# A wide state-space layer: its first norm on one copy of each token, the residual sum moved one stage on

## The chip, the cores and the metric

The kernel runs on one core of a Trainium2 chip. The metric is the device time of one execution in microseconds (us), from start to end, on that core; lower is better. The engines are named as in the profile: PE (matrix multiplication; PEld are its weight loads), DVE (vector), ACT (activation functions and copies out of PSUM), POOL (general elementwise work, which reads and writes SBUF), and SP, which here only issues DMAs. Each engine runs its own instructions in order; semaphores order the engines among each other.

## The reference

The input is `x` of 4 images x 64 channels x 128 x 128 pixels, in float32. Four layers follow one another. Only the last one is touched; in it each image is a sequence of 16,384 tokens with 64 features:

```python
y = relu(conv2d(x, conv1_w, conv1_b)); y = conv2d(y, conv2_w, conv2_b)
t = y.reshape(Bn, C, Hh * Ww).transpose(0, 2, 1)
t = t + mamba(layernorm(t, ln1_w, ln1_b), ...)
t = t + pvt2ffn(layernorm(t, ln2_w, ln2_b), Hh, Ww, ...)
y = t.transpose(0, 2, 1).reshape(Bn, C, Hh, Ww)
return x + y          # x: the layer's own input
```

`mamba` projects the normalised tokens to 128 inner channels and 128 gates, runs a causal depthwise convolution of 4 taps and silu over the sequence, derives a step size delta (softplus) and, for each token, 64 numbers B and 64 numbers C, and then for each of the 128 x 64 (channel, state) pairs runs the recurrence

```python
h = h * exp(delta * A) + (delta * u) * B
y = sum over states of h * C
```

before it multiplies by silu(gate) and projects back to 64 features. `pvt2ffn` is a feed-forward block: 64 to 256 features, a 3 x 3 depthwise convolution, gelu, back to 64.

## The kernel before

Five functions run one after the other: `layer0` (a small state-space layer with 16 states), `layer1`, `layer2_convs3` (which ends with the two convolutions of the last layer; it writes the layer's input to the DRAM tensor x3 and the tokens to t3), `layer3_mamba` (t3 to s3 and n3) and `layer3_ffn` (n3 and s3 to the output).

**`layer3_mamba`** cuts the tokens into 64 chunks of TC = 1024. Channels lie on the partitions. A chunk is 16 groups of 4 states, each group 4 iterations, so 64 iterations per chunk and 4096 in all. In each iteration (`_Mamba.run`) DVE runs one scan (L626) over a 128 x 1024 tile: the decay `da` comes from ACT (L582), the input `bx` from PE in PSUM, the result goes into one of 8 ring slots. POOL multiplies the ring slot by C (L632, tile `cb`, loaded by DMA, L421). PE adds the products of a group up into `y` (L457) some 3 iterations after the group's last scan; only then is the ring slot free for the scan 8 iterations later. There are two kinds of group. For kind A (10 of 16) ACT (L431) and POOL (L435) prepare scaled copies which PE transposes into `bx` (L514). For kind D (6 of 16) PE spreads B over the partitions (L520) and DVE multiplies `bx` by `du` (L526). PSUM holds three `bx` tiles and one `y` tile; the helper steps below `take` one of the three and `give` it back, which leaves the scans two.

**The order** is fixed by the program: each engine's instructions stay in the order in which they are written (`_Pin`). The helper steps for the next chunk (`ahead`) and for the last one (`behind`) are generators. `yield m.slot(c, name)` continues at the end of a given iteration; `yield "next", 0` continues in the next iteration. Counted within a chunk of 64, the steps stand at: project 9, centre2 11, norm2 13 (of the chunk just ended), centre 21, norm 23, conv 32, z 34, v 36, duT 43, C 53, B 55 (of the next chunk).

**`ahead`** is the first norm. The convolution on PE treats two taps at once: rows 0 to 63 of its input S hold the tokens shifted by one column against rows 64 to 127, which hold them as they are. The kernel before loads t3 twice into X, shifted and unshifted (L1353 or L1356, and L1357), and norms both copies: centring matmul (L300 with K.cent), copy with scale and square on ACT (L1375, L1376), mean matmul, logarithm and exponential (L140, L141), and a product on POOL into S (L1385), all of them on 128 x 1024 elements. Two columns are carried from chunk to chunk in `tail` (L1365, L1388). `front` then runs convolution (L300 with cw), gate and step size.

**`behind`** loads the tokens t3 and the layer's input x3 of the finished chunk, projects y and adds the tokens in PSUM (L672), copies the sum (L1402), adds x3 on POOL (L1404), norms again on 128 x 512 elements (two halves of the 1024 tokens on the two halves of the partitions; L1411, L1412, L140, L141, L1421), and stores tokens plus x3 in s3 (L1423) and the normed tokens in n3 (L1424).

**`layer3_ffn`** works in 32 strips of 16 image rows. Per strip it loads n3 (with `first`) and s3 (`res`), runs the depthwise convolution partly on PE (L1584) and partly on DVE (L1530), and adds `res` at the end (L1551). POOL sets border columns there and nothing else. Its tiles have two buffers.

All DMAs concerned are issued by SP, in program order; a DMA that has to wait stops those behind it.

Of the kernel before, what the change touches and what calls it, by code (L numbers as in the profile page):

```python
# [10 lines left out]
F32 = mybir.dt.float32  # L11
# [6 lines left out]
P = 128  # L18
B, C, HH, WW = 4, 64, 128, 128
HW = HH * WW  # L20
TC = 1024
NH = TC // 512
# [89 lines left out]
def _halves(ap, t0):  # L112

    return [ap[:, t0 + 512 * h : t0 + 512 * (h + 1)] for h in range(NH)]
# [660 lines left out]
def _gradients(ctx, tc, K, x1, out):  # L775
# [9 lines left out]
    with tc.tile_pool(name="sob", bufs=2) as sp, tc.tile_pool(name="sobc", bufs=1) as sc, tc.tile_pool(  # L785
# [5 lines left out]
        for b in range(B):  # L791
            img = x1[b].rearrange("c (h r w) -> (c h) r w", h=2, w=C)
            for r0 in range(0, HH, R):
                X = sp.tile([P, R + 2, C], F32, name="X", tag="X")
                h = sp.tile([P, R + 2, C + 1], F32, name="h", tag="h")
# [8 lines left out]
                for i, e in ((at, mid), (mid, to)):  # L804
                    nc.sync.dma_start(X[:, i:e, :], img[:, lo + i - at : lo + e - at, :])
                    nc.scalar.copy(h[:, i:e, 0:1], X[:, i:e, 0:1])
                    nc.scalar.copy(h[:, i:e, C : C + 1], X[:, i:e, C - 1 : C])
# [519 lines left out]


@with_exitstack
def layer3_mamba(ctx, tc, K, w, t3, x3, s3, n3):  # L1330

    nc = tc.nc
    slots = {"centre": -43, "norm": -41, "conv": -32, "z": -30, "v": -28, "B": -9, "duT": -21, "C": -11}
    slots |= {"project": 73, "centre2": 75, "norm2": 77}
    m = _Mamba(ctx, tc, K, 64, w, "DADAADAADADAADAA", {"xc": 1, "sz": 2, "tmp": 4, "bc": 1, "soon": (8, 20, 52), "da": 7, "made": 7}, slots)
    cp = m.cp
    eps = cp.tile([P, 1], F32, name="eps3")
    nc.vector.memset(eps, 1e-5)
    woT = cp.tile([P, 64], F32, name="woT")
    nc.sync.dma_start(woT, w["out_wT"])  # L1340

    g1, b1 = (_dup(nc, cp, w[k], f"{k}_") for k in ("ln1_w", "ln1_b"))
    m.shift(b1)
    pad = cp.tile([P, 1], F32, name="pad")
    nc.vector.tensor_scalar_mul(pad, b1, -1.0)

    tail = cp.tile([P, 2], F32, name="tail")

    def load(c):
        b, t0 = c["at"]  # L1350
        X = c["X"] = m.t("X", 1)
        if t0:
            nc.sync.dma_start(X[:64], t3[b, :, t0 - 1 : t0 - 1 + TC])  # L1353
        else:
            nc.gpsimd.memset(X[:64, 0:1], 0.0)  # L1355
            nc.sync.dma_start(X[:64, 1:], t3[b, :, : TC - 1])  # L1356
        nc.sync.dma_start(X[64:], t3[b, :, t0 : t0 + TC])  # L1357

    def ahead(c):
        if c is chunks[0]:  # L1360
            load(c)
        t0 = c["at"][1]
        S = m.t("S", 1, TC + 2)
        if t0:
            nc.gpsimd.tensor_copy(S[:, :2], tail)  # L1365
        else:
            nc.gpsimd.tensor_copy(S[:, :2], pad.to_broadcast([P, 2]))
        xs, sq = m.tmp("nxc"), m.tmp("nsq")
        yield m.slot(c, "centre")
        pm = m.take()  # L1370
        m.mm(pm, (K.cent, c["X"]))
        if c is not chunks[-1]:
            load(chunks[c["no"] + 1])
        yield "next", 0
        nc.scalar.activation(xs, pm, AF.Copy, scale=g1)  # L1375
        nc.scalar.activation(sq, pm, AF.Square)  # L1376
        m.give(pm)
        yield m.slot(c, "norm")
        pm = m.take()
        m.mm(pm, (K.j2, sq))  # L1380
        yield "next", 0
        _rstd(nc, sq, pm, eps)
        m.give(pm)
        yield "next", 0
        nc.gpsimd.tensor_mul(S[:, 2:], xs, sq)  # L1385
        if not t0:
            nc.gpsimd.tensor_copy(S[:64, 2:3], pad[:64])
        nc.gpsimd.tensor_copy(tail, S[:, TC:])  # L1388
        yield from m.front(c, S, lambda: None)

    def behind(c, yg):
        b, t0 = c["at"]
        tx = m.tmp("tx")
        tr, xr = tx[:, :512], tx[:, 512:]
        for h in range(NH):
            nc.sync.dma_start(tr[64 * h : 64 * (h + 1)], _halves(t3[b], t0)[h])
            nc.sync.dma_start(xr[64 * h : 64 * (h + 1)], _halves(x3[b], t0)[h])
        yield m.slot(c, "project")
        pm = m.take(1)
        m.project(pm, woT, yg, tr)  # L1400
        yield "next", 0
        nc.scalar.copy(tr, pm)  # L1402
        m.give(pm)
        nc.gpsimd.tensor_add(xr, xr, tr)  # L1404
        yield m.slot(c, "centre2")
        pm = m.take(1)
        m.mm(pm, (K.cent, tr))
        yield "next", 0
        no = m.tmp("no")
        xs, o = no[:, :512], no[:, 512:]  # L1410
        nc.scalar.copy(xs, pm)  # L1411
        nc.scalar.activation(o, pm, AF.Square)  # L1412
        m.give(pm)
        yield m.slot(c, "norm2")
        pm = m.take(1)
        m.mm(pm, (K.j2, o))
        yield "next", 0
        _rstd(nc, o, pm, eps)
        m.give(pm)
        yield "next", 0  # L1420
        nc.gpsimd.tensor_mul(o, xs, o)  # L1421
        for h in range(NH):
            nc.sync.dma_start(_halves(s3[b], t0)[h], xr[64 * h : 64 * (h + 1)])  # L1423
            nc.sync.dma_start(_halves(n3[b], t0)[h], o[64 * h : 64 * (h + 1)])  # L1424

    chunks = [{"at": (b, t0), "reset": t0 == 0} for b in range(B) for t0 in range(0, HW, TC)]
    m.run(chunks, ahead, behind, 48)


@with_exitstack  # L1430
def layer3_ffn(ctx, tc, K, w, n3, s3, out):

# [1 line left out]
    nc = tc.nc  # L1436
    R = 16
    HR = (R + 2) // 2
    NK = R // 8
    half = [slice(64 * h, 64 * (h + 1)) for h in range(2)]  # L1440
    cp = ctx.enter_context(tc.tile_pool(name="ffc", bufs=1))
    wp = ctx.enter_context(tc.tile_pool(name="ffw", bufs=2))
# [121 lines left out]
    for n, (b, r0) in enumerate(strips):  # L1564
        simg = s3[b].rearrange("c (r w) -> c r w", w=WW)
        h0 = H[0]
        H = {}
        ahead = first(*strips[n + 1], H) if n + 1 < len(strips) else iter(())
        next(ahead, None)

        res = wp.tile([P, NK, 4, WW], F32, name="res3", tag="res3")
        for q in range(R // 4):
            nc.sync.dma_start(res[half[q % 2], q // 2], simg[:, r0 + 4 * q : r0 + 4 * q + 4, :])

        g0 = [wp.tile([P, NK, 4, WW], F32, name=f"g0{i}", tag=f"g0{i}") for i in range(2)]
        o = wp.tile([P, NK, 4, WW], F32, name="o3", tag="o3")
        for kk in range(NK):
            pd = [dp.tile([P, 4, WW], F32, name=f"pd{i}", tag=f"pd{i}") for i in range(2)]
            for k in range(9):
                dy, dx = divmod(k, 3)  # L1580
                for h in range(2):
                    r = 8 * kk + 4 * h + dy
                    for i in range(2):
                        nc.tensor.matmul(  # L1584
                            pd[i][half[h]],
                            diag[half[i], k, :],
                            h0[half[i], r : r + 4, dx : dx + WW],
                            start=k == 0,
                            stop=k == 8,
                        )  # L1590
                if k % 3 == 2:
                    next(ahead, None)
                if (kk, k) == (0, 3) and owed:
                    second(*owed)
                    more(rest, 1)
                if (kk, k) == (1, 3):
                    second(n, g0, g1, res, o, 0)
                    more(rest, 4)
                pin()
            for i in range(2):  # L1600
                nc.scalar.activation(g0[i][:, kk], pd[i], AF.Gelu, bias=dwb[:, i : i + 1])
            if not kk:
                nc.scalar.activation(g1, g1, AF.Gelu, bias=dwb1)
                rest = taps(H[1]) if 1 in H else iter(())
                g2 = more(rest, 4)
            pin()
        owed, g1 = (n, g0, g1, res, o, 1), g2
# [59 lines left out]
@with_exitstack  # L1667
def kernel(ctx, tc, w, cst, x, out):
    nc = tc.nc
    dp = ctx.enter_context(tc.tile_pool(name="dram", bufs=1, space=DRAM))  # L1670
    x1, x2, x3, t3, s3, n3 = (
        dp.tile([B, C, HW], F32, name=f"d_{n}") for n in ("x1", "x2", "x3", "t3", "s3", "n3")
    )
    for upto, layer, *of in (
        ("sel", layer0, w["l0"], x, x1),
        (None, layer1, w["l1"], x1, x2),
        (None, layer2_convs3, w["l2"], w["l3"], x2, x3, t3),
        ("sel", layer3_mamba, w["l3"], t3, x3, s3, n3),
        ("eye", layer3_ffn, w["l3"], n3, s3, out),
    ):  # L1680
        with tc.tile_pool(name="const", bufs=1) as kp:
            layer(tc, _Consts(nc, kp, cst, upto), *of)
# [26 lines left out]
```

## Time and profile before

| what | us |
|---|---|
| median of 3 runs | 17,647.88 (17,646.33 to 17,652.58) |
| profiled execution, its own time | 17,656.56 |
| its span, first to last instruction | 17,654.7 |
| first to last scan of `layer3_mamba` | 5,501.8 to 16,689.3 |
| from one chunk to the next, mean (median) | 174.9 (174.5) |

| per chunk of `layer3_mamba` | rows of the profile |
|---|---|
| scan L626, DVE, 64 times | 2327 ns each, one every 2.25 us |
| multiplication L526, DVE, 24 times | 1209 ns each, one every 1.12 us |
| ring product L632, POOL, 64 times | 2382 ns each, one every 2.3 us |
| first norm, ACT: L1375, L1376, L140, L141 | 1115, 1016, 1101, 1058 ns |
| first norm, POOL: L1385, L1388, L1365 | 2419, 185, 190 ns |
| residual sum, POOL: L1404 | 1290 ns |

The span is that of the profiled execution; its own time is 1.9 us longer, and the median of the other runs 8.7 us shorter. An instruction's duration overlaps the next one's start a little, so that on a full engine the distance of two starts is the better price.

### The profile page before, as it was taken

The page shows a single profiled execution, that of the slowest core. Times are in us where ns is not written, and L with a number is a line of the kernel's source. Part 1 is how long each engine was busy: PE and PEld are TensorE (multiplying, and loading weights), DVE is VectorE, ACT ScalarE, POOL GpSimd, SP SyncE. Part 2 cuts the span into 40 slices and gives each one's busy share as a digit, 9 for nine tenths or more (in the row PEclk, how much of TensorE's full clock was granted, in tenths as well). Part 3 has the DMA queues.
Part 4 walks back from the last instruction along what each step waited for, and adds up shares of the span by engine and source line. Part 5 has one row for each costly group of instructions (what it writes and reads, how often), then busy time and mean ns, then how long its engine had stood idle before and what let it go on. Part 6 is the DMA issues. An engine that isn't in the chain of part 4 may idle for free. (4 is left out here: it accounts for less than half of the span.)

```text
span 17654.7 us, 242673 instructions
## 1 busy us (share of the span) xinstructions
PE 14230.1 (81%) x82490; PEld 6984.1 (40%) x82490; DVE 15333.9 (87%) x8623; ACT 14311.2 (81%) x29985; POOL 13820.2 (78%) x7966
## 2 busy tenths in 40 slices
PE   7888888798997777777777777777777777777799
PEld 3333333387334333333333333333333333333333
DVE  8999999522216999999999999999999999999977
ACT  8999999112335999999999999999999999999733
POOL 7999999200005999999999999999999999999700
PEclk8888888799998999999999999999999999999899
DMA  6766666111212333333333333333333333333222
GB/s 160 179 179 178 175 179 177 51 61 45 72 41 79 89 90 91 88 93 85 93 85 94 83 95 84 94 86 91 87 91 86 93 87 91 89 90 91 69 59 55
DMA packets 669699, 1723.23 MB, mean 98 GB/s; under 512 B 196816, under 2 KB 232096, under 8 KB 661024
## 3 DMA queue, kind: packets, MB, share of 16 engines
q1 hardware_dynamic: 668448, 1707.69, 36.0%
q8 instruction: 646, 10.58, 0.3%
q14 instruction: 605, 4.96, 0.1%
HBM read 1434.33 MB, written 272.63 MB: 97 GB/s over the span
## 5 line engine op out<-in xcount | busy, mean ns | idle before, releaser
L632 POOL TENSOR_TENSOR ring<-ring,cb 128x1024 f32<-128x1024 f32 x5120 | 12038.9, 2381 | 335.4 <-DVE ring L626 186.1
L626 DVE TENSOR_TENSOR_SCAN ring<-da,state,bx 128x1024 f32<-128x1024 f32 x4848 | 11053.0, 2327 | 70.8 <-PE y L457 38.1
L431 ACT ACTIVATE bxT<-duT,BT 128x128 f32<-128x128 f32 x21504 | 6706.0, 389 | 29.9 <-PE bx L514 28.1
L582 ACT ACTIVATE da<-dl,A 128x1024 f32<-128x1024 f32 x5120 | 5751.0, 1139 | 168.1 <-DVE ring L626 115.2
L514 PE MATMUL bx<-cst,bxT 128*128 128x128 f32 x24576 | 3693.7, 300 | 945.1 <-DVE ring L626 641.6
L514 PEld LDWEIGHTS bx<-cst,bxT 128*128 128x128 f32 x24576 | 3248.7, 209 | 2341.9 <-DVE ring L626 1523.1
L520 PE MATMUL bx<-bc,spread 64*128 64x512 f32 (+1 forms) x8192 | 2401.2, 684 | 1439.2 <-DVE ring L626 1427.9
L457 PE MATMUL y<-ring,cst 128*32 128x512 f32 x20480 | 3030.3, 675 | 120.8 <-POOL ring L632 120.1
L526 DVE TENSOR_TENSOR bx<-du,bx 128x1024 f32<-128x1024 f32 x2048 | 2463.1, 1211 | 301.3 <-PE bx L520 183.8
L520 PEld LDWEIGHTS bx<-bc,spread 64*128 64x128 f32 (+1 forms) x8192 | 690.2, 195 | 2819.0 <-DVE ring L626 2305.6
L457 PEld LDWEIGHTS y<-ring,cst 128*32 128x32 f32 x20480 | 633.3, 119 | 2040.0 <-issue 1433.7
L1197 PE MATMUL cv<-img,cw 64*64 64x512 f32 x9216 | 1009.3, 595 | 73.2 <-DMA img<-d_x 45.5
L300 PE MATMUL bx<-S,cw 128*128 128x512 f32 x1024 | 663.2, 806 | 367.9 <-DVE ring L626 354.5
L1355 POOL MEMSET X<- 64x1 f32 x4 | 0.4, 97 | 1122.2 <-DMA cw<-in_l_conv_wT 1122.2
L435 POOL TENSOR_TENSOR bxT<-duT,BT 128x512 f32<-128x512 f32 x768 | 808.3, 1053 | 10.1 <-ACT BT L381 10.1
L1122 POOL TENSOR_TENSOR xs<-xs,cl 128x1024 f32<-128x1024 f32 x32 | 76.0, 2374 | 860.8 <-DVE cl L1121 860.8
L1496 POOL MEMSET h<- 128x18 f32 x64 | 8.3, 132 | 875.2 <-PE pd L1584 443.5
L1197 PEld LDWEIGHTS cv<-img,cw 64*64 64x64 f32 x9216 | 435.1, 134 | 645.5 <-issue 537.8
L1510 ACT ACTIVATE h<-ph,ff_fc_b 128x384 f32<-128x384 f32 (+1 forms) x384 | 201.1, 578 | 593.2 <-PE ph L1505 593.2
L1584 PE MATMUL pd<-h,diag 64*64 64x512 f32 x4608 | 632.0, 603 | 0.7 <-issue 0.7
L626 DVE TENSOR_TENSOR_SCAN ring<-da,bx 128x1024 f32<-128x1024 f32 x272 | 604.8, 2268 | 9.4 <-PE y L457 5.8
L1530 DVE SCALAR_TENSOR_TENSOR g<-h,dww,g 128x2048 f32<-128x2048 f32 x256 | 601.9, 2351 | 11.0
(314 smaller groups left out, 9963.3 us busy)
## 6 DMA issues: line engine op xcount, KB each, us to landing
cb<-c SPq DMA_DIRECT2D x5120, 128.0 KB, 2.8
dl<-d SPq DMA_DIRECT2D x2048, 128.0 KB, 3.3
du<-d SPq DMA_DIRECT2D x2048, 128.0 KB, 3.7
d<-pos SPq DMA_DIRECT2D x128, 512.0 KB, 3.7
d<-u SPq DMA_DIRECT2D x128, 512.0 KB, 3.9
X<-d_t SPq DMA_DIRECT2D x124, 256.0 KB, 4.1
S<-in_x SPq DMA_DIRECT2D x120, 256.5 KB, 4.5
res<-in_x SPq DMA_DIRECT2D x128, 128.0 KB, 3.0
```

The costliest lines, as they stand in the source:

```text
L300: self.nc.tensor.matmul(out[: l.shape[1], k : k + 512], l, r[:, k : k + 512], start=i == 0, stop=i == len(pairs) - 1)
L431: nc.scalar.activation(t[:, k, q].rearrange("p e j -> p (e j)"), c["duT"][:, k, :], AF.Copy, scale=c["BT"][:, k, n : n + 1])
L435: nc.gpsimd.tensor_mul(t[:, k].rearrange("p q e j -> p q (e j)"), c["duT"][:, k].unsqueeze(1).to_broadcast(shape), c["BT"][:, k, NQ * g : ...
L457: nc.tensor.matmul(c["y"][DD * j : DD * (j + 1), _COLS[h]], K.sel, hc[:, _COLS[h]], start=False, stop=u["g"] == self.ng - 1,)
L514: nc.tensor.transpose(bx[:, P * m : P * (m + 1)], v["bxT"][:, m, :, :, j].rearrange("p q e -> p (q e)"), self.K.eye)
L520: nc.tensor.matmul(bx[:, _COLS[h]], self.spread[v["g"]][r], self.rows(v["c"]["B"], h, 0), start=True, stop=True)
L526: nc.vector.tensor_mul(tiles[k], v["c"]["du"][j], tiles[k])
L582: nc.scalar.activation(das[nexp], v["c"]["dl"][k], AF.Exp, scale=self.A[:, k, v["g"] : v["g"] + 1])
L626: nc.vector.tensor_tensor_scan(hs, das.pop(i), tiles[i], 0.0 if u["c"].get("reset") else st, ALU.mult, ALU.add)
L632: nc.gpsimd.tensor_mul(hc, hs, u["cb"])
L1197: nc.tensor.matmul(p[i][half[h]], W[half[i], k, :], src[half[i], at : at + 4, dx : dx + WW], start=k == 0, stop=k == 8,)
L1584: nc.tensor.matmul(pd[i][half[h]], diag[half[i], k, :], h0[half[i], r : r + 4, dx : dx + WW], start=k == 0, stop=k == 8,)
```

## The change

**First norm (`ahead`).** Each token is loaded and normed once. X becomes 128 x 512: the first 512 tokens on partitions 0 to 63, the next 512 on partitions 64 to 127. Centring, scaling, squaring, mean, logarithm, exponential and the product run on 512 columns and end in the tile `nx` (one buffer of the shared kind `tmp` where there were two). The norm takes a half of a PSUM tile. S then gets 3 leading columns from `tail` and is filled by four DMAs from SBUF to SBUF, each of 64 partitions x 512 columns: both halves, once for each of the two shifts. `tail` is taken from the last columns of `nx` by two small copies. The DMAs are issued two iterations after POOL's product.

**Residual sum.** `layer3_mamba` no longer reads x3; s3 holds the tokens without it. `layer3_ffn` loads x3 beside s3 (four DMAs a strip, tile `xin`) and POOL adds the two, 128 x 1024 elements a strip.

```diff
-    tail = cp.tile([P, 2], F32, name="tail")
+    tail = cp.tile([P, 3], F32, name="tail")
+    nc.vector.memset(tail, 0.0)
...
-        X = c["X"] = m.t("X", 1)
-        if t0:
-            nc.sync.dma_start(X[:64], t3[b, :, t0 - 1 : t0 - 1 + TC])
-        else:
-            nc.gpsimd.memset(X[:64, 0:1], 0.0)
-            nc.sync.dma_start(X[:64, 1:], t3[b, :, : TC - 1])
-        nc.sync.dma_start(X[64:], t3[b, :, t0 : t0 + TC])
+        X = c["X"] = m.t("X", 1, 512)
+        for h, src in enumerate(_halves(t3[b], t0)):
+            nc.sync.dma_start(X[64 * h : 64 * (h + 1)], src)
...
-        S = m.t("S", 1, TC + 2)
-        if t0:
-            nc.gpsimd.tensor_copy(S[:, :2], tail)
-        else:
-            nc.gpsimd.tensor_copy(S[:, :2], pad.to_broadcast([P, 2]))
-        xs, sq = m.tmp("nxc"), m.tmp("nsq")
+        S = m.t("S", 1, TC + 3)
+        no = m.tmp("nx")
+        xs, sq = no[:, :512], no[:, 512:]
         yield m.slot(c, "centre")
-        pm = m.take()
+        pm = m.take(0)
...
         yield m.slot(c, "norm")
-        pm = m.take()
+        pm = m.take(0)
         m.mm(pm, (K.j2, sq))
...
-        nc.gpsimd.tensor_mul(S[:, 2:], xs, sq)
-        if not t0:
-            nc.gpsimd.tensor_copy(S[:64, 2:3], pad[:64])
-        nc.gpsimd.tensor_copy(tail, S[:, TC:])
+        nc.gpsimd.tensor_mul(xs, xs, sq)
+        nc.gpsimd.tensor_copy(S[:, :3], tail if t0 else pad.to_broadcast([P, 3]))
+        for h in range(2):
+            nc.gpsimd.tensor_copy(tail[64 * h : 64 * (h + 1), : 3 - h], xs[64:, 509 + h :])
+        yield "next", 0
+        yield "next", 0
+        for k in range(2):
+            for h in range(NH):
+                at = 3 - k + 512 * h
+                nc.sync.dma_start(S[64 * k : 64 * (k + 1), at : at + 512], xs[64 * h : 64 * (h + 1)])
         yield from m.front(c, S, lambda: None)
...
-        tx = m.tmp("tx")
-        tr, xr = tx[:, :512], tx[:, 512:]
+        tr = m.tmp("tx")[:, :512]
         for h in range(NH):
             nc.sync.dma_start(tr[64 * h : 64 * (h + 1)], _halves(t3[b], t0)[h])
-            nc.sync.dma_start(xr[64 * h : 64 * (h + 1)], _halves(x3[b], t0)[h])
...
-        nc.gpsimd.tensor_add(xr, xr, tr)
...
-            nc.sync.dma_start(_halves(s3[b], t0)[h], xr[64 * h : 64 * (h + 1)])
+            nc.sync.dma_start(_halves(s3[b], t0)[h], tr[64 * h : 64 * (h + 1)])
...
+        ximg = x3[b].rearrange("c (r w) -> c r w", w=WW)
+        xin = wp.tile([P, NK, 4, WW], F32, name="xin", tag="xin")
         for q in range(R // 4):
             nc.sync.dma_start(res[half[q % 2], q // 2], simg[:, r0 + 4 * q : r0 + 4 * q + 4, :])
+            nc.sync.dma_start(xin[half[q % 2], q // 2], ximg[:, r0 + 4 * q : r0 + 4 * q + 4, :])
+        nc.gpsimd.tensor_add(res, res, xin)
```

More of the change, by code (lines that the diff above doesn't have):

```diff
@@ L1329, in layer3_mamba @@
 @with_exitstack
-def layer3_mamba(ctx, tc, K, w, t3, x3, s3, n3):
+def layer3_mamba(ctx, tc, K, w, t3, s3, n3):
     nc = tc.nc
@@ L1430, in layer3_ffn @@
 @with_exitstack
-def layer3_ffn(ctx, tc, K, w, n3, s3, out):
+def layer3_ffn(ctx, tc, K, w, n3, s3, x3, out):
     nc = tc.nc
@@ L1677 @@
         (None, layer2_convs3, w["l2"], w["l3"], x2, x3, t3),
-        ("sel", layer3_mamba, w["l3"], t3, x3, s3, n3),
-        ("eye", layer3_ffn, w["l3"], n3, s3, out),
+        ("sel", layer3_mamba, w["l3"], t3, s3, n3),
+        ("eye", layer3_ffn, w["l3"], n3, s3, x3, out),
     ):
```

## The prediction

> **What bounds the kernel now.** I read three things in this order: the page's slices, to find the stage that the change touches; the table of stretches, to see which engine is full there; and the waits and the timelines of that engine, to see what is left to gain. The page shows the long flat stretch of the state-space layer (slices 13 to 38):
>
> ```profile
> PE 14230.1 (81%) x82490; PEld 6984.1 (40%) x82490; DVE 15333.9 (87%) x8623; ACT 14311.2 (81%) x29985; POOL 13820.2 (78%) x7966
> ...
> DVE  8999999522216999999999999999999999999977
> ```
>
> From the first scan of layer 3 to its last, and over the feed-forward part after it, the stretches say:
>
> ```profile
> 5501.80:16689.30 11187.50, 8634.78 (x47534) 4228.37 (x47534) 11002.75 (x5693) 10582.48 (x23206) 10792.68 (x6140) 0.91 0.33 89
> ...
> 16800.00:17655.00 855.00, 837.69 (x5710) 258.11 (x5708) 678.74 (x392) 303.96 (x496) 12.86 (x126) 0.99 0.24 57
> ```
>
> The columns are length, then busy PE, PEld, DVE, ACT, POOL, clock, DMA share. In the first row DVE works 11,002.75 of 11,187.5 us. Its work is fixed: per chunk 64 scans, 24 multiplications and one gating. So the most that any edit off DVE can win there is the idle rest, 185 us (2.9 us in each of 64 chunks). In the second row PE is full (98%) and POOL empty. The waits of DVE between 6000 and 16000 us name that rest:
>
> ```profile
> DVE bx L526 <- PE bx L520: 107.5, 119, 1.4
> DVE ring L626 <- PE y L457: 37.8, 64, 1.1
> DVE ring L626 <- PE bx L514: 7.1, 30, 0.6
> DVE ring L626 <- POOL S L1385: 3.4, 11, 0.3
> ```
>
> DVE waits for PE. Whether the change helps depends on why PE is late. I numbered the scans of a chunk 0 to 63 and added the timeline's DVE idle by position over 61 chunks. Per chunk: 0.29 us before scan 20, 0.03 at 12, 0.03 at 24, 0.02 at 26, 0.05 at 27, 0.40 at 28, 0.90 at 32, 0.77 at 35, 0.33 at 48; total with crumbs 2.88. One typical chunk, around positions 27 to 35, first POOL, then PE, then DVE:
>
> ```profile
> 8023.32 2.45 POOL L1385 TENSOR_TENSOR S<-nxc,nsq 128x1024 f32<-128x1024 f32 x1
> 8025.84 0.18 POOL L1388 COPY tail<-S 128x2 f32<-128x2 f32 x1
> 8025.98 2.39 POOL L632 TENSOR_TENSOR ring<-ring,cb 128x1024 f32<-128x1024 f32 x1
> 8028.33 1.04 POOL L435 TENSOR_TENSOR bxT<-duT,BT 128x512 f32<-128x512 f32 x1
> 8029.33 4.68 POOL L632 TENSOR_TENSOR ring<-ring,cb 128x1024 f32<-128x1024 f32 x2
> 8033.95 0.19 POOL L634 COPY state<-ring 128x4 f32<-128x4 f32 x1
> ```
>
> ```profile
> 8021.82 2.19 PE L514 MATMUL bx<-cst,bxT 128*128 128x128 f32 x16 [1.22 <-ACT nsq L140]
> 8023.94 1.93 PE L457 MATMUL y<-ring,cst 128*32 128x512 f32 x16
> ...
> 8034.06 1.90 PE L457 MATMUL y<-ring,cst 128*32 128x512 f32 x10 [1.28 <-POOL ring L632]
> 8035.89 1.99 PE L520 MATMUL bx<-bc,spread 64*128 64x512 f32 x8
> 8040.60 5.40 PE L300 MATMUL bx<-S,cw 128*128 128x512 f32 x8 [2.72 <-DVE ring L626]
> ```
>
> ```profile
> 8025.96 6.82 DVE L626 TENSOR_TENSOR_SCAN ring<-da,state,bx 128x1024 f32<-128x1024 f32 x3 [0.45 <-PE y L457]
> ...
> 8037.07 1.23 DVE L526 TENSOR_TENSOR bx<-du,bx 128x1024 f32<-128x1024 f32 x1 [0.92 <-PE bx L520]
> ```
>
> POOL has no gap at all here. It is behind: at 8034.06 PE has to wait 1.28 us for POOL's ring product before it may add up y, the spread matmul behind it in PE's queue is late, and DVE loses 0.92 us. Before that, PE lost 1.22 us to ACT's logarithm, which held a PSUM tile; y ran late and scan 28 lost 0.45 us waiting for its ring slot. The gap at 20 has the same form (PE waits up to 1.45 us for POOL at 7826). So about 1.7 of the 2.88 us come from POOL and ACT running behind.
>
> [...]half the columns should cost about half; the trace agrees, 2.42 us at 1024 columns and 1.27 to 1.29 at 512. [...]the trace shows the queueing (POOL stands 1.64 us a chunk before the residual sum while ring products follow it). [...]128 KB issues here land in 2.4 to 4.2 us, none from SBUF to SBUF. [...]the clock record shows half clock from 8041.78 to 8045.20, after the 2.72 us pause, just when the convolution runs.
>
> **The change, part by part (per chunk).**
> - ACT: four passes over 1024 columns (1115, 1016, 1101, 1058 ns) become 512 columns; the second norm's rows give 580, 601, 671, 635. 4.29 to 2.49 us: -1.80.
> - PE: the centring and mean matmuls halve: 125.0/63 + 118.6/63 = 3.87 to 1.93: -1.93.
> - POOL: out go L1385 (2.42), L1365 (0.19), L1388 (0.19) and L1404 (1.29), 4.08; in come a 512-column product (1.28) and three copies of at most 3 columns (0.18 each), 1.83: -2.25. With L1404 goes its wait for ACT, 1.64.
> - SP: out two loads of x3, in four placements; at 0.6 us an issue +1.2. Bytes: X 512 to 256 KB, x3 256 to 0, placements 512: the same 768 KB.
> - DVE: nothing but one memset.
> - PSUM: the norm takes a half tile, but a whole one stays blocked; it comes back earlier by the shorter PE and ACT work.
>
> **On the path.** POOL's lag (end of product minus end of scan, median by position) is 2.5 us at its floor, 4.1 at position 10 where it stands before the sum, 4.5 at 12, 7.5 at 18, 4.3 at 22, 8.5 at 27. Without sum and wait it leaves position 12 at 2.5 to 2.8, that is 1.7 earlier, and at 22 is about at its floor (4.3-1.7=2.6). More than the 1.45 that PE waits before 20: that gap (0.29) goes. At the norm POOL gains another 0.96 (2.79 out, 1.83 in), so it is 2.5 ahead at position 31. The gap at 32 needs 1.3 (0.85 to start y no later than 8033.2, and 0.45 since DVE comes sooner): it goes, 0.90. ACT frees the tile 0.43 to 1.4 sooner and PE's mean matmul is 0.95 shorter: the gaps at 24 to 28 (0.51) go, 12 (0.03) too. Sum 1.73; I keep 1.65, because 0.1 of crumbs stays. The gaps at 35 and 48 (1.09) stay: before the convolution PE waits for DVE's tile, not for POOL, and they come from half-clock phases. Late next is PE itself, half-clocked. 64 x 1.65 = 106 us. Ends: 1.0 (the first rival) and 2.4, if the half-clock phases fall elsewhere.
>
> **Hidden parts.** The placements: the copies end near 8024, four issues take 2.3, landing at most 4.2: 8030.5. The convolution starts at 8040.6, so 10 us cover them; uncovered they would cost up to 6.5 us a chunk. Behind them in SP's queue is the next C load, which waits for POOL until 8033.95 anyway. Unmeasured is an SBUF-to-SBUF landing: 2.4 to 13.3 us (the slowest X load). Prologue: nothing hides there; PE -3.1, ACT -1.8, POOL -0.9 against +6 for placing (2.3 of issues, 3.7 of landing): about zero, 2 us either way. Feed-forward: 32 sums of 2.4 us on a POOL that works 13 of 855 us, beside a full PE; memsets of the next strip stand behind each sum, but its loads go out a strip (27 us) ahead; only the first strip can wait, 0 to 9 us. Its SP gains 4 issues (2.4 us) of 27. I take 2 us.
>
> Net: -106 + 2 = -104. The profiled execution, 17,656.56 (span 17,654.7), becomes 17,552.6; the median of the runs, 8.7 lower, 17,544.
>
> **Rivals.**
> - Half of it. The sum on POOL sits beside DVE-rich positions 8 to 11, where POOL has idle time (1.05 at 9), so removing it may be worth nothing later. Then only 0.96 arrives at 31: 0.40+0.10 and 0.55 of the gap at 32, 1.0 us, 64 us: 17,584. Against it: from position 12 to 54 POOL's gaps come to 0.05 us.
> - No change. PE gets longer pauses before the convolution, so half clock strikes there in every chunk and the gaps at 35 and 48 grow by what the others lose. For it: a 1.05 us gap at 35 stands in three chunks of four. Against: those rarely have both. 17,648.
> - Slower: the placements land late. PE stands at the convolution, and with it all tiles of DVE. Decisive point: a landing 1.65 us after PE is ready, near 8042, 18 us after the copies. Were it 21, each chunk would lose 3: 64 x (3-1.65) = +86: 17,734. For it: SP stands up to 13 us behind waits in other places. Against: in this place none.
> - That the sum moves no work off the path is the first rival; POOL work does fall in any case.
>
> **How the numbers follow.** Likeliest 0.67 (gains 75 to 140: 17,508 to 17,573), half 0.18, no change 0.08, slower 0.07. 0.2%, or 35 us, is what can be told from no change. Half and likeliest are both faster: 0.85. The range takes the half case with a margin and the upper end of 2.4 us: 17,490 to 17,620.
>
> **What would show it.** Right: a chunk of 173.2 us instead of 174.9; no DVE gap at 20, 28, 32, those at 35 and 48 still there; POOL's wait before L1404 gone and 6.0 us of idle time at about 6.6; the convolution's matmul still waiting for DVE. Wrong: PE waiting there for a DMA into S, or clock phases that move the gaps instead of removing them.

## The result and the profile after

The changed kernel takes 17,579.31 us (median of 5 runs, 17,575.63 to 17,582.30) against 17,649.74 before: a ratio of 0.9959, 95% interval 0.9945 to 0.9974. It is faster by 70 us, or 0.4%. The forecast was 104 us faster, with a range from 17,490 to 17,620.

In the profiled executions the span went from 17,654.7 to 17,579.1 us, by 75.6. First scan to last scan of `layer3_mamba` accounts for 74.2 of them; the feed-forward part after the last scan is 4.6 us longer (965.4 to 970.0), and what lies before the first scan 5.9 shorter. Stretches of the kernel after, with the columns of the same view of before; the first row is first scan to last scan, the second the feed-forward part:

```profile
5495.80:16609.20 11113.40, 8517.94 (x47282) 4157.08 (x47282) 10975.32 (x5694) 10470.24 (x23207) 10665.99 (x6134) 0.91 0.33 89
16725.00:17579.00 854.00, 830.98 (x5676) 256.43 (x5668) 730.36 (x389) 303.21 (x496) 91.34 (x155) 0.99 0.32 74
```

PE, ACT and POOL all worked less in the first row, as forecast. DVE is still idle for 138 us of it. The waits of DVE between 6000 and 16000 us (who waited for whom, us in total, times, longest):

```profile
DVE bx L526 <- PE bx L520: 117.6, 64, 2.2
DVE ring L626 <- DVE bx L526: 0.5, 1, 0.5
DVE ring L626 <- issue: 0.4, 2, 0.3
```

The waits for y, for transposes and for POOL are gone. The one for the spread matmul (L520) is as large as before (107.5), but no longer in several places. Added up by position over 61 chunks, DVE's idle time is now 0.04 us a chunk before scan 32 and 2.10 before scan 35. Before, 35 had 0.77. Here is that place in a typical chunk; POOL first, around the norm, then PE, then DVE:

```profile
7999.77 1.32 POOL L1379 TENSOR_TENSOR nx<-nx 128x512 f32<-128x512 f32 x1
8001.00 0.21 POOL L1380 COPY S<-tail 128x3 f32<-128x3 f32 x1
8001.27 0.41 POOL L1382 COPY tail<-nx 64x3 f32<-64x3 f32 x2
8001.76 2.38 POOL L632 TENSOR_TENSOR ring<-ring,cb 128x1024 f32<-128x1024 f32 x1
```

```profile
8009.01 2.74 PE L457 MATMUL y<-ring,cst 128*32 128x512 f32 x16
8011.68 1.13 PE L520 MATMUL bx<-bc,spread 64*128 64x512 f32 x4
8013.56 1.13 PE L520 MATMUL bx<-bc,spread 64*128 64x512 f32 x4 [0.75 <-DVE ring L626]
8016.93 6.67 PE L300 MATMUL bx<-S,cw 128*128 128x512 f32 x8 [2.24 <-DVE ring L626]
8023.52 1.13 PE L520 MATMUL bx<-bc,spread 64*128 64x512 f32 x4
```

```profile
8017.89 4.58 DVE L626 TENSOR_TENSOR_SCAN ring<-da,state,bx 128x1024 f32<-128x1024 f32 x2
8024.70 1.23 DVE L526 TENSOR_TENSOR bx<-du,bx 128x1024 f32<-128x1024 f32 x1 [2.22 <-PE bx L520]
```

PE hardly waits for POOL in front of y (L457) any more: 2.5 us between 6000 and 16000 us, where it was 104.5. But the convolution (L300) takes 6.67 us where it took 5.40 in the chunk shown before (in 18 of 61 chunks before it took 3.70), the spread matmul behind it comes late, and DVE loses 2.22 us. The stretches around it, cut at the boundaries of the clock record, say why; the second column is PE's busy time, the value ahead of the last two the granted clock:

```profile
8012.70:8016.10 3.40, 1.23 (x6) 0.30 (x4) 3.40 (x3) 3.40 (x10) 3.40 (x2) 1.00 0.02 7
8016.10:8019.50 3.40, 2.58 (x3) 1.17 (x4) 3.40 (x3) 3.40 (x8) 3.40 (x4) 0.50 0.00 0
8019.50:8022.90 3.40, 3.40 (x5) 1.35 (x4) 2.98 (x2) 1.64 (x3) 3.40 (x3) 0.50 0.52 154
8022.90:8026.30 3.40, 3.40 (x22) 0.71 (x20) 1.50 (x2) 2.67 (x7) 3.40 (x2) 1.00 0.00 0
```

The clock record of this trace changes only at steps of 3.413 us. After the first step here, in which PE was busy for 36% (1.23 of 3.40 us), the granted clock was 0.50 for two steps, and all of the convolution but its last 0.7 us falls into them; in the chunk shown before the change it was one step. I counted this over 61 chunks: each of the 371 falls to half clock followed a step in which PE was busy for at most 53%, and each return to full clock a step with at least 84%. One more thing stands out. Most chunks now last 174.08 us, to 0.02: exactly 51 such steps (51 x 3.4133 = 174.08). Before, four chunks lasted 699.7, which is 205 steps.

My theory: the chunk is held in step with the clock's steps, called windows below. Time that is won elsewhere moves the convolution against the windows until more of it runs at half clock. The rival is the plain sum: each wait is worth its length, and the wait at 35 is PE's own work.

The trace of the changed kernel shows how the chunk is held. From the fourth to the ninth chunk of the first image the convolution starts 1.16, 0.97, 0.87, 0.83, 0.81 and 0.80 us after the boundary of a step. It takes 6.50, 6.59, 6.64, 6.66, 6.67 and 6.67 us, and these chunks last 173.90, 173.99, 174.04, 174.06, 174.07 and 174.08 us. Each of these chunks but the last was shorter than 51 steps, the next convolution started earlier in its step by about as much, more of that convolution ran at half clock, and its chunk was longer, until nothing moved any more.

### The profile page after: what moved, and what is told of

Its sections match the earlier page's. It is cut to its first block, busy times and chain, and to the rows that moved or that the text cites. A ratio compares the mean times of both kernels' runs of the same rounds, so it can differ in the third digit from the quotient of the medians.

```text
span 17579.1 us, 242686 instructions
## 1 busy us (share of the span) xinstructions
PE 14106.9 (80%) x82234; PEld 6965.8 (40%) x82234; DVE 15366.1 (87%) x8624; ACT 14196.0 (81%) x29985; POOL 13778.3 (78%) x7990
## 5 line engine op out<-in xcount | busy, mean ns | idle before, releaser
L520 PE MATMUL bx<-bc,spread 64*128 64x512 f32 (+1 forms) x8192 | 2395.8, 679 | 1570.9 <-DVE ring L626 1564.8
L457 PE MATMUL y<-ring,cst 128*32 128x512 f32 x20480 | 2914.5, 680 | 10.4 <-POOL ring L632 10.4
L520 PEld LDWEIGHTS bx<-bc,spread 64*128 64x128 f32 (+1 forms) x8192 | 675.6, 192 | 2989.0 <-DVE ring L626 2526.3
L457 PEld LDWEIGHTS y<-ring,cst 128*32 128x32 f32 x20480 | 618.8, 120 | 1807.2 <-issue 1380.4
L300 PE MATMUL bx<-S,cw 128*128 128x512 f32 x1024 | 758.1, 907 | 340.7 <-DVE ring L626 327.3
L1379 POOL TENSOR_TENSOR nx<-nx 128x512 f32<-128x512 f32 x64 | 83.6, 1306 | 1150.0 <-ACT nx L141 1150.0
L1197 PEld LDWEIGHTS cv<-img,cw 64*64 64x64 f32 x9216 | 490.0, 134 | 590.7 <-issue 482.0
L1527 DVE SCALAR_TENSOR_TENSOR g<-h,dww,g 128x2048 f32<-128x2048 f32 x256 | 660.6, 2581 | 11.5 <-DVE g L1527 0.5
L1574 POOL TENSOR_TENSOR res<-res,xin 128x1024 f32<-128x1024 f32 x32 | 88.4, 2761 | 708.2 <-DMA xin<-d_x 596.6
L300 PEld LDWEIGHTS bx<-S,cw 128*128 128x128 f32 x1024 | 288.8, 297 | 804.3 <-DVE ring L626 437.0
```

The lines of the kernel that those rows point to most:

```text
L300: self.nc.tensor.matmul(out[: l.shape[1], k : k + 512], l, r[:, k : k + 512], start=i == 0, stop=i == len(pairs) - 1)
L457: nc.tensor.matmul(c["y"][DD * j : DD * (j + 1), _COLS[h]], K.sel, hc[:, _COLS[h]], start=False, stop=u["g"] == self.ng - 1,)
L520: nc.tensor.matmul(bx[:, _COLS[h]], self.spread[v["g"]][r], self.rows(v["c"]["B"], h, 0), start=True, stop=True)
L1197: nc.tensor.matmul(p[i][half[h]], W[half[i], k, :], src[half[i], at : at + 4, dx : dx + WW], start=k == 0, stop=k == 8,)
L1527: nc.vector.scalar_tensor_tensor(g1, tap, wk, g1, ALU.mult, ALU.add)
```

## The experiments

All times are medians beside the kernel before on the same chip (17,648 to 17,649 there).

**One part alone.** The first kernel keeps the sum as before, the second keeps the norm as before:

```diff
# the norm alone, against the changed kernel (loads and store of the sum go with it)
-        nc.gpsimd.tensor_add(res, res, xin)        # layer3_ffn
+        nc.gpsimd.tensor_add(xr, xr, tr)           # layer3_mamba
...
# the sum alone, against the changed kernel (the rest of the norm goes with it)
-        X = c["X"] = m.t("X", 1, 512)
+        X = c["X"] = m.t("X", 1)                   # both copies normed on 1024 columns
```

> The norm on 512 columns and its placement alone; the residual sum stays where it was before. Theory (clock): the changed kernel's chunk of 174.08 us is 51 windows of 3.413 us, in which the PE clock is set, and the wait before scan 35 grows until a chunk fills them. Then one part alone, which leaves the other waits at some 0.5 us a chunk, runs the same chunk of 174.1 us: 17,575 us, 5 below the changed kernel, since the feed-forward part does not pay for x3. Rival (two parts that add): each part is worth about half: 17,615 us.

> The residual sum moved alone; the norm stays as before on 1024 columns. Theory (clock): POOL comes 1.7 us sooner, the waits before scans 20 and 32 go, the one before 28 stays (0.45), and the wait before 35 grows up to 2.3: chunk 174.1 us, 17,580 us like the whole change. Rival (two parts that add): 17,615 us. Rival of the prediction (the sum is worth nothing, since POOL has spare time there): 17,650 us.

Measured: 17,588.59 for the norm alone (ratio 0.9966, 0.9952 to 0.9979) and 17,608.50 for the sum alone (0.9977, 0.9967 to 0.9986). They win 60 and 40 us, together 100, while both at once give 70. So the parts don't add. The first is 14 us above its number, the second 28. In both kernels the median chunk lasts 174.07 to 174.08 us, though their waits stand in different places. DVE's waits, first the norm alone, then the sum alone:

```profile
DVE bx L526 <- PE bx L520: 102.1, 111, 1.5
DVE ring L626 <- PE y L457: 1.2, 2, 0.6
```

```profile
DVE ring L626 <- PE y L457: 71.4, 63, 1.6
DVE bx L526 <- PE bx L520: 35.8, 70, 0.8
```

By position the norm alone has 0.99 us before 20, 0.79 before 32 and 0.11 before 35; the sum alone 1.21 before 48 and 0.51 before 32. I had expected both to lose the time before 35. With the norm alone the convolution ran at full clock, 3.70 us in all 61 chunks. The theory of a held chunk stands, that of a fixed place does not. The largest waits, at 20 in the first kernel and at 48 in the second, follow a half-clocked step within 12 us in 55 of 57 and in 61 of 61 cases, so there the half clock took another place that was tight. The waits at 32 don't: ahead of them PE waits for POOL's ring product (1.18 and 0.93 us), as before the change. Of the 28 us of the sum alone, some 19 lie in the first two chunks of the images, 173.0 and 175.1 in most of them where the whole change has 170.0 and 172.9, and 6 ahead of the first scan.

**Filling the pause.** Two matmuls with zero weights, which add zeros to y, go in front of the convolution, into the 2.3 us in which PE waits for DVE:

```diff
         yield self.slot(c, "conv")
+        for k in range(2):      # or 1; shortened: none in the first chunk; y: the tile of the chunk that runs
+            nc.tensor.matmul(y[:, _COLS[k % NH]], zero, K.t[:, :512], start=False, stop=False)
         pm = self.take()
```

> The changed kernel with two matmuls of 128 x 512 more a chunk, whose weights are zero and which add nothing to y, in front of the convolution, in the 2.3 us in which PE waits for DVE there. Theory (clock): PE is no longer idle in that window, the convolution runs at full clock in 3.7 us instead of 6.7, the wait before scan 35 falls from 2.1 to 0.1 us: chunk 172.0, 17,470 us. Rival (the convolution is simply long for PE): more PE work helps nothing, 17,579 us or, where the matmuls run over the pause, up to 60 us more.

> The changed kernel with one zero-weight matmul of 128 x 512 in front of the convolution instead of two, about 0.85 us of the pause of 2.28. Windows after which the clock was halved had PE busy for 0.53 of their length at most, this one would have 0.58 or more. Theory (a window's busy share decides): as good as two, 17,490 us. Rival (the array must be busy up to the convolution): half or less, 17,535 us or more.

> The changed kernel with the same two zero-weight matmuls, placed eleven iterations earlier, in front of the centring matmul of the norm, and not in the pause before the convolution. Theory (clock in the pause decides): the convolution stays at half clock and the chunk at 174.1 us: 17,580 us, within 15. Rival (more PE work anywhere keeps the clock up): 17,490 us.

> The kernel before with the same two matmuls in front of the convolution. Theory (clock): its wait before scan 35 (0.77 us a chunk) falls to 0.1, those that come from POOL and ACT (1.7) stay: chunk 174.2, 17,605 us. Rival (POOL and ACT alone set the chunk): 17,650 us.

Measured: 17,487.76 with two (ratio 0.9908, 0.9895 to 0.9922), 17,486.60 with one (0.9908, the same interval), 17,580.03 with the two in another place, 17,603.90 with two in the kernel before (0.9975, 0.9964 to 0.9985). All four went as the clock theory said; the first is 18 us short of its number. More work for PE made the kernel 92 us faster where it stood in the pause, and changed nothing (0.7 us) where it did not. In the kernel before, where the wait at 35 is 0.77 us and not 2.10, it is worth 45 us. PE and then DVE's waits in the kernel with one zero matmul (L364; the profile has two records for one such matmul; lines are shifted, and L531 is the spread matmul):

```profile
7993.27 1.13 PE L531 MATMUL bx<-bc,spread 64*128 64x512 f32 x4 [0.82 <-DVE ring L637]
7994.32 1.12 PE L364 MATMUL y<-cst,zero 128*128 128x512 f32 x2
7996.64 3.70 PE L300 MATMUL bx<-S,cw 128*128 128x512 f32 x8 [1.19 <-DVE ring L637]
```

```profile
DVE bx L537 <- PE bx L531: 7.9, 35, 0.5
DVE ring L637 <- PE bx L525: 2.6, 16, 0.2
```

The convolution takes 3.70 us instead of 6.67, and of DVE's 118 us of waits 11 stay. The number of falls to half clock did not drop (389 instead of 371 in 61 chunks); they lie elsewhere, where DVE hardly waits for PE. Nor is this kernel free of the steps: its chunks alternate between 171.73 and 173.01 us, and two of them last 344.74, which is 101 steps, so what the matmul won is half a step in each chunk. With the chunks at the start of an image the average is 172.16 us. The one-matmul kernel is the best of this study, 93 us faster than the change and 162 faster than the kernel before.

**Filling the pause with one part alone.** Both kernels with one part get the two matmuls as well.

> The norm alone (sum where it was before) with the two zero-weight matmuls in front of the convolution. Without them its convolution ran at full clock, and its waits stood before scans 20 and 32 (0.99 and 0.79 us a chunk). Theory (filling the pause helps only where the half clock meets the convolution): nothing gained: 17,588 us, within 20. Rival (the matmuls are worth some 90 us by themselves): 17,500 us.

> The residual sum moved alone, with the two zero-weight matmuls in front of the convolution. Without them its waits stood before scans 48 (1.21) and 32 (0.51 us a chunk), and 0.19 at 35. Theory (filling the pause helps only where the half clock meets the convolution): nothing gained: 17,608 us, within 20. Rival (the matmuls are worth some 90 us by themselves): 17,520 us.

Measured: 17,588.55 and 17,595.97 (ratios 0.9966, 0.9954 to 0.9979, and 0.9971, 0.9960 to 0.9982). Nothing gained with the norm alone, 12.5 us with the sum alone, most of it in the chunks where an image begins. Both stay at 174.07 to 174.08 a chunk. So the 92 us are not the matmuls' own. They are there in full only where both parts have cleared the other tight places, and where the half clock meets the convolution.

**More work for DVE.** If the chunk is held, a little more work on DVE must cost little. One instruction a chunk in front of scan 10, whose result isn't used:

```diff
+            if i % per == 10:
+                nc.vector.tensor_scalar_mul(more, more, 1.0)         # first 128 x 1024, then 128 x 256
+                nc.vector.tensor_mul(more, tiles[i][:, :512], more)  # third kernel, in its place
```

> The changed kernel with one more DVE instruction a chunk, a multiplication of a 128 x 1024 tile in SBUF by 1, in front of scan 10: about 0.6 us of the engine that bounds the stage, 38 us in 64 chunks. Theory (the chunk is held at 51 windows of the clock): the wait before scan 35 shrinks from 2.3 to 1.7 us and the chunk stays at 174.08: 17,579 us, within 10. Rival (DVE's work adds to DVE's waits): 17,617 us.

> As the run with one more DVE instruction a chunk, but on 128 x 256. The one on 128 x 1024 took 2.04 us and not 0.6, more than a chunk of 51 windows can take up (171.9 + 2.0 = 173.9, and its waits have a floor); this one should take 0.5 to 0.6, 32 to 38 us in 64 chunks. Theory (the chunk is held at 51 windows): the wait before scan 35 shrinks by as much, the chunk stays at 174.08: 17,579 us, within 10. Rival (DVE's work adds to DVE's waits): 17,611 us or more.

> The changed kernel with one more DVE instruction a chunk again, now a product of a 128 x 512 tile with one half of a bx tile in PSUM, the kind of operand that L526 has; half of its 1.12 us, some 0.6, 38 us in 64 chunks. The two others took 2.04 and 1.64 us and added 82 and 67: with the 1.05 us that one half-clocked window costs at scan 35, 171.7 + 2.04 + 1.05 = 174.8 and 171.7 + 1.64 + 1.05 = 174.4, both above 174.08. Now 171.7 + 0.6 + 1.05 = 173.4 lies below. Theory (below 174.08 the chunk is held there): the wait before scan 35 shrinks from 2.1 to 1.5 us, the time stays at 17,579 us, within 10. Rival (no hold, DVE's work adds): 17,617 us.

Measured: 17,661.50, 17,646.38 and 17,593.36. The first two expectations failed, because the added work was far larger than meant: the 0.6 us for 128 x 1024 was my estimate, near the 0.69 us that another one-input operation of DVE on an SBUF tile of that size takes in the trace of before (L1121). The rows of the three, in this order:

```profile
L624 DVE TENSOR_SCALAR more<-more 128x1024 f32<-128x1024 f32 x64 | 130.4, 2037 | 0.0
```

```profile
L624 DVE TENSOR_SCALAR more<-more 128x256 f32<-128x256 f32 x64 | 105.0, 1641 | 0.0
```

```profile
L624 DVE TENSOR_TENSOR more<-bx,more 128x512 f32<-128x512 f32 x64 | 43.3, 677 | 0.0
```

By the distance of scans 9 and 10 (3.37 us without them) they cost 1.96, 1.57 and 0.60 us a chunk, so 126, 100 and 38 us. The time grew by 82, 67 and 14. In the first two the wait at 35 shrank to 0.93 and 1.15, about the 1.05 that stood there in the kernel before with one half-clocked step. The third amount lay in the range where the chunk should be held. It is nearly: chunks alternate between 173.39 and 174.77 us, two of them 348.16, which is 102 steps; the profiled span grew by 7.0 us and the median by 14, not by 38. I had said within 10. That the chunk is held at whole steps is shown by seven kernels with the same median of 174.07 to 174.08 and three different sets of waits (at 35 alone; at 20 and 32; at 48 and 32). Other kernels keep other whole numbers: 101 steps in two chunks with the pause filled, 154 in three (525.65 us) with the first of these additions. The loop that holds the chunk is shown for the wait at 35, by the phases of the changed kernel given above; for the waits at 20 and 48 it is argued.

**Late placing.** The four transfers into S are issued one iteration before the convolution:

```diff
-        yield "next", 0
-        yield "next", 0
+        yield "at", c["no"] * m.ng * ND + m.slots["conv"] - 1
```

> The changed kernel with the four placing transfers issued one iteration before the convolution, not five, behind one more load of C in SP's queue. They should land near 8016.2 on the traced chunk's clock (issues from 8011.6 for 2.3 us, landing 2.4), when PE reaches the convolution at 8016.9. Theory (10 us of cover were there and are not needed): 17,579 us, within 15. Rival (the placing is what delays the convolution): later by what the transfers are later, 100 us or more.

Measured: 17,570.22 (ratio 0.9950, 0.9937 to 0.9962). In the change the last landing that the trace has lies 11.7 us before the convolution starts (median; 9.5 at least), here 0.7 us (0.1 at least), and nothing is lost. The traces have the landing of only half of these transfers. The slower rival is excluded for this queue: no PE matmul waited for S between 6000 and 16000 us. The runs of this kernel scatter more than others (17,525.81 to 17,581.02). Its trace holds two periods: most chunks last 174.08 us, but nine chunks of the second image come in threes of 172.66, 172.89 and 173.27, together 518.82 us or 152 steps. How often a run keeps the shorter period may be what scatters; the other runs have no trace.

## Why the prediction was right, and where it was off

**The side and the range** were right, 35 us from the forecast, near the first rival's number (17,584) but not for its reason. That rival said that the sum moved off POOL would be worth nothing; the sum alone is worth 40 us. The time lies outside the likeliest case (17,508 to 17,573), and inside the range only because the range was drawn to take in this rival. So the range held in part by luck.

**The price of each part** held. Four ACT passes take 669, 579, 674 and 631 ns: 2.55 us a chunk, forecast 2.49. POOL's product takes 1.31 us (1.28), the three copies 0.57 (0.54). POOL's lag at position 12 fell from 4.5 to 2.9 us (2.5 to 2.8), at 22 from 4.3 to 2.8 (2.6), at 27 from 8.5 to 6.3. At 31 it fell by 1.6 (7.25 to 5.65), not by the 2.5 that I gave (my two terms, 1.7 and 0.96, make 2.7); 1.3 was needed there. The waits before 12, 20, 24, 26, 27, 28 and 32 (1.73) came down to 0.04: the chain POOL, y, spread matmul, DVE was read rightly, though at 20 half of the 18 waits of before also followed a half-clocked step.

**The step that failed** is "The gaps at 35 and 48 (1.09) stay". The one at 48 went (0.33 won). The one at 35 rose from 0.77 to 2.10 (1.33 lost). That was the second rival's mechanism, half clock at the convolution in every chunk; I had given it a chance of 0.08 and made it all or nothing, where it took back 1.33 of the 2.06 us won. The sum, per chunk: 1.73 + 0.33 - 1.33 is 0.73 of waits (with crumbs 0.71), yet a chunk became 1.17 shorter. The other 0.46 I had not priced. With the same instructions DVE's busy time fell from 11,002.75 to 10,975.32 us, 0.43 a chunk: each wait also exposes the end of the instruction before it, which the next one otherwise overlaps (a scan lasts 2.33 us at a distance of 2.25, a multiplication 1.21 at 1.12). DVE's idle gaps of any length fell from 5.7 to 2.3 a chunk, and 3.4 of them at 0.08 to 0.09 us make about 0.3, an estimate; what the rest is stays open. So 1.65 was the forecast and 1.17 came, and without the part that was not priced it would have been 0.71.

**The feed-forward part** was forecast at +2 us within 0 to 9 and took 4.6, by another way than the first strip. POOL's sum meets DVE's depthwise taps, which read two SBUF tiles. The taps before (L1530) and after (L1527), and POOL's sum:

```profile
L1530 DVE SCALAR_TENSOR_TENSOR g<-h,dww,g 128x2048 f32<-128x2048 f32 x234 | 550.2, 2351 | 10.2
```

```profile
L1527 DVE SCALAR_TENSOR_TENSOR g<-h,dww,g 128x2048 f32<-128x2048 f32 x235 | 607.3, 2584 | 10.6 <-DVE g L1527 0.5
...
L1574 POOL TENSOR_TENSOR res<-res,xin 128x1024 f32<-128x1024 f32 x29 | 80.2, 2767 | 651.9 <-DMA xin<-d_x 540.3 <-DVE g L1527 111.6
```

About one tap a strip is stretched from 2.35 to 4.33 us while the sum runs, 57 us more for DVE in the strips of these rows. A full PE hides it, but where an image begins: there PE waits for DVE's border rows of N, 18.3 us in all instead of 12.3. With the norm alone, which has no sum there, the part takes 965.8.

**The prologue** was forecast at zero, 2 us either way, and came out 5.9 us shorter: the first convolution starts at 5,457.15 instead of 5,463.06. The placing there took 3.6 us, from the first issue (5,453.51) to the convolution, and not 6.

**What would show it**: no wait at 20 and 28, POOL's wait for ACT gone, 6.9 us of POOL idle time a chunk (6.6 said), the convolution waiting for DVE and not for a transfer, all as written; a chunk of 173.7 instead of 173.2, and at 35 a longer wait, the clock phases that I had named among the signs of being wrong.

## What to carry to other kernels

In a loop that PE does not bound, look at the clock record beside the waits. Here PE was busy for 36% of a 3.413 us step, with a pause of 2.24 us across its end; the matmul that followed took 6.67 us at half clock instead of 3.70, and 1.33 of the 2.06 us won in other places of each chunk were lost there. That matmul feeds the engine that is full, and a zero-weight matmul in the pause was worth more (92 us) than the change itself (70); in the kernel before it was worth 45, with one part alone 0 and 12. And where a chunk, or a few chunks together, last a whole number of clock steps, single waits should not be summed: test an edit together with the filled pause before judging it.

## What the runs showed of the hardware

- In the changed kernel each of 371 falls to half clock came after a step of 3.413 us with PE busy for at most 53%, and each return after one with at least 84%; in the kernel before, 373 falls came after at most 53% too. These shares are counts, not limits: in the kernel before 29 steps at full clock and at most 53% were followed by no fall, with the sum alone 95, and there falls came after up to 57%. A convolution of eight passes took 3.70, 5.40 or 6.67 us with no half-clocked step, one, or most of two in it. With one zero-weight matmul in the pause it took 3.70 us in all 61 chunks.
- Chunks came mostly in whole numbers of these steps: 51 steps for one chunk in seven kernels, 101 or 102 for two, 154 for three and 205 for four in others.
- An SBUF-to-SBUF transfer of 64 rows x 2 KB lands in 2.4 us (median; 2.2 to 4.3, for the half of the transfers whose landing the trace has), where the 128 KB issues from and to DRAM took 2.4 to 4.2 in the kernel before (medians by tile).
- DVE's multiplication of a 128 x 256 SBUF tile by a constant took 1.64 us with POOL at work, where a product with a PSUM operand on twice the columns took 0.68. In all 64 chunks it began within the run of a POOL ring product, mostly 0.86 us after its start, and ended 0.15 us after that product's end (0.55 for the 128 x 1024 tile), while the one with the PSUM operand ended ahead of it. Why it took so long was not shown.
